# A four-layer kernel's start: the group norm's factors spread by TensorE, eight input buffers, later loads for the second layer, and a first step on VectorE

## The chip, the cores and the metric

One core of a Trainium2 chip runs the whole kernel. The metric is device time in microseconds (us), the median of runs; all values are float32.

## What is computed

The input `x` is 8 images of 16 channels and 128 by 128 points. Four layers follow, each adding its result to what went in, after a group norm (8 groups of two channels). The change concerns the first, an attention layer:

```
x = x + L0(gn(x))                       # then L1, L2, L3 in the same way
# L0, for each point: T = 3 tokens of 48 numbers (the 3x3 patch, wrapped at the edges)
x = fold(in_x); h = ln(x); q, k, v = split(h @ w_attn.T)     # 4 heads of 12
att = softmax(q k / sqrt(12)); x = x + (att v) @ w_proj.T
x = x + gelu(ln(x) @ w_fc.T) @ w_fcp.T
out = conv_w . sum over tokens of ln(x) + conv_b
```

The second layer (16 by 16 products with gates made from means and maxima) needs the weights `w1_0` to `w1_4` and the vectors `b1_0` to `b1_4`.

## The kernel before

**Start.** ScalarE's queue issues one load of constants, then `rep` (L168) and the loop at L219 issue 96 small loads: biases and second-layer weights, each repeated for 8 images. Meanwhile SP's queue loads the input in eight pieces `xj` of 1 MB into two buffers (L236 to L240), and VectorE takes statistics of each (`bn_stats`, L242). `group_stats` (L178) makes from them, per channel and image, the factor `rs` and the shift `d`: aggregate, two small TensorE products (`pm`, `pv`), a square root on ScalarE (L197), and a few VectorE operations. Only then is the table `const0` loaded (L246).

**The factors.** L263 to L275 write `rs` and `d` to DRAM (`aff_d`) and read them back with 24 loads in the layout that the products need, as `aff`. L308 to L324 make `wcen`, the centring weights of four pairs of images, with `aff` in them: four rounds of a POOL memset, two VectorE copies, one TensorE product (`pb`) and one VectorE operation, with two buffers. The layer's own weights (`wqkv`, `wfc`, `wcv`, `wpc`, `wfq`, `wfp`) are loaded on ScalarE's and SP's queues; `centered` (L290) takes the mean off three of them on VectorE.

**The steps.** The layer is worked in 32 steps of four image rows (`Step`, L403). The loop at L656 overlaps them: in turn n, `ahead` (step n + 2) loads its rows into the single buffer `xin` (24 loads, 32 for step 0) and is centred, `then` (n + 1) gets q, k, v, products and scores, `new` (n) attends, projects and starts its hidden layer, `old` (n - 1) ends its hidden layer, `done` (n - 2) is stored (`store`, L584, which loads `xl` first). In the turns n = -2, -1 and 0 only some of these exist, so step 0 has no other step's work beside it.

- `multiply` (L464): q times shifted k, on POOL, eight operations of 3 or 2 x 512 numbers per partition into the five buffers `large`.
- `scores` (L479): TensorE sums them by head into PSUM bank 1, the fifth score into bank 0, which also holds the variances that `Variances.finish` (L392) reads.
- `softmax` (L490), then `attend` (L511), 12 times: three TensorE products spread the weights into banks 1 to 3, VectorE multiplies by v (L518), and POOL adds two of each three results to the first (L527).
- `project` (L529) needs the sums of two k.

[...] `in_turn` (L210) fixes the order of the instructions it is given on each engine as written; the rest is put in place by a scheduler from the program's order. Every load signals one of eight landing semaphores, taken in turn over both queues, and waits until the semaphore's load before it has landed.

Of the kernel before, what the change touches and what calls it, by code (L numbers as in the profile page):

```python
# [9 lines left out]
F32 = mybir.dt.float32  # L10
# [3 lines left out]
PSUM = bass.MemoryType.PSUM  # L14
# [3 lines left out]
BC = B * C  # L18
# [3 lines left out]
NP = B // 2  # L22
# [14 lines left out]
def _constants():  # L37
    g, r = (a.reshape(-1) for a in np.mgrid[0:2, 0:E])
    token = 64 * g + r
    h, c = r // HD, r % C  # L40
    parts = {}
    center = np.zeros((128, 64))
    center[token, r] = 1.0
    center[token, :E] -= 1.0 / E
    parts["center"] = center

    halfvar = np.zeros((128, 62))
    halfvar[token, 30 + g] = -0.5 / E
    parts["halfvar"] = halfvar
    score = np.zeros((128, 56))  # L50
    score[token, 24 + 4 * g + h] = 1.0
    parts["score"] = score
    spread = np.zeros((128, 4, 128))
    bcast = np.zeros((128, 5, 128))
    last = np.zeros((128, 3, 128))
    for t in range(4):
        bcast[32 * t + 16 + g, 4, token] = 1.0
        for n in range(4):
            bcast[32 * t + 4 * (n // 2) + 2 * (n % 2) + g, n, token] = 1.0
            spread[32 * t + 8 * n + 4 * g + h, n, token] = 1.0  # L60
    for k in range(4):
        for u in range(3):
            v = 32 * (2 * (k % 2) + u % 2) + 8 + 4 * (u // 2) + 2 * (k // 2)
            last[v + g, u, 32 * k + 16 * g + c] = 1.0
    parts["spread"] = spread.reshape(128, 512)
    parts["bcast"] = bcast.reshape(128, 640)
    parts["last"] = last.reshape(128, 384)
    p = np.arange(BC)
    parts["pair"] = 0.5 * (p[:, None] // 2 == p[None, :] // 2)


    parts["chan"] = 1.0 * (p[:, None] % 4 == np.arange(4)[None, :])
    gather = np.zeros((128, 2, 2, 32))
    for g in range(2):
        gather[p, 0, g, g * 16 + p % C] = -1.0
        gather[p, 1, g, g * 16 + p % C] = 2.0
    parts["gather"] = gather.reshape(128, 128)
    parts["image"] = 1.0 * (p[:, None] // C == np.arange(B)[None, :])
    parts["basis"] = 3 * (3.5 - (p // C)[:, None])

    copies = np.zeros((128, 2, 128))
    for g in range(2):
        for j in range(8):
            copies[p, g, j * C + p % C] = p // C % 2 == g
    parts["copies"] = copies.reshape(128, 256)
    at, where = 0, {}
    for name, a in parts.items():
        where[name] = (a.shape[0], at, at + a.shape[1])
        at += a.shape[1]
    out = np.zeros((128, at), np.float32)  # L90
    for name, a in parts.items():
        n, lo, hi = where[name]
        out[:n, lo:hi] = a
    return out, where
# [6 lines left out]
def kernel(  # L101
# [63 lines left out]
    eps_t = cpool.tile([128, 1], F32, name="eps")  # L165
    nc.gpsimd.memset(eps_t, EPS)

    def rep(vec, n, name):  # L168

        t = cpool.tile([n * C, 1], F32, name=name)  # L170
        for b in range(n):
            nc.scalar.dma_start(t[b * C : (b + 1) * C], vec.unsqueeze(1))
        return t

    bias0 = rep(b0_conv, B, "bias0")
# [34 lines left out]
    def in_turn(engine, ins):  # L210

        if engine in chain:
            tc.add_manual_dep(ins, chain[engine].name, order, reason="in turn")
        chain[engine] = ins
        return ins
# [3 lines left out]
    for n in range(5):  # L219
        t = cpool.tile([BC, BC], F32, name=f"w1_{n}")  # L220
        nc.gpsimd.memset(t, 0.0)
        for b in range(B):
            r = slice(b * C, (b + 1) * C)
            nc.scalar.dma_start(t[r, r], w1[n].rearrange("i o -> o i") if n < 2 else w1[n])
        w1s.append(t)
        b1s.append(rep(b1[n], B, f"b1_{n}"))

# [5 lines left out]
    x1d = dram.tile([BC, HW], F32, name="x1d")  # L233
    with ExitStack() as l0:
        wp = l0.enter_context(tc.tile_pool(name="w0", bufs=1))
        with tc.tile_pool(name="x0", bufs=2) as xp:  # L236
            bn0 = xp.tile([BC, NCH, 6], F32, name="bn0", bufs=1)
            for j in range(8):
                t = xp.tile([BC, HW // 8], F32, name="xj")
                nc.sync.dma_start(t, xv[:, bass.ts(j, HW // 8)])  # L240
                for i in range(NCH // 8):
                    nc.vector.bn_stats(bn0[:, NCH // 8 * j + i], t[:, bass.ts(i, 512)])  # L242
            mean0, _, rs0, d0 = group_stats(bn0, "0")
        lo, hi = _WHERE["center"][1], _WHERE["last"][2]
        const0 = wp.tile([128, hi - lo], F32, name="const0")
        nc.scalar.dma_start(const0, const_in[:, lo:hi])  # L246

        def k0(name):
            _, a, z = _WHERE[name]
# [7 lines left out]
        def zeros(shape, name):  # L257
            t = wp.tile([128, *shape], F32, name=name)
            nc.gpsimd.memset(t, 0.0)
            return t  # L260


        aff_d = dram.tile([BC, 2], F32, name="aff_d")  # L263
        aff_s = wp.tile([BC, 2], F32, name="aff_s")
        nc.vector.tensor_copy(aff_s[:, 0:1], rs0)
        nc.vector.tensor_copy(aff_s[:, 1:2], d0)
        nc.sync.dma_start(aff_d, aff_s)
        aff = zeros([2, NP], "aff")
        for a in range(2):
            src = aff_d[:, a : a + 1].rearrange("(d p g c) a -> p g c (d a)", p=2, g=2, c=C)  # L270
            for odd in range(2):
                for g in range(2):
                    for i in range(3):
                        r = 64 * (g ^ odd) + 16 * i
                        nc.sync.dma_start(aff[r : r + 16, a, odd::2], src[odd, g])  # L275


        wqkv = zeros([3, 64], "wqkv")
# [2 lines left out]
        for i in range(3):  # L281
            for g in range(2):
                r = slice(64 * g + i * 16, 64 * g + i * 16 + 16)
                nc.scalar.dma_start(
                    wqkv[r, :, :E], w0_qkv[i].rearrange("c (n o) -> c n o", n=3)
                )
                nc.sync.dma_start(wfc[r], w0_fc[i])
                nc.scalar.dma_start(wcv[r, g * 16 : (g + 1) * 16], w0_conv[i])

        def centered(t):  # L290
# [6 lines left out]

        wpc, wfp, wfq = (zeros([64], name) for name in ("wpc", "wfp", "wfq"))
        for g in range(2):
            nc.sync.dma_start(wpc[64 * g : 64 * g + E, :E], w0_proj)  # L300
            nc.scalar.dma_start(wfq[64 * g : 64 * g + 64, :E], w0_fcp[128:192])
        nc.scalar.dma_start(wfp[:, :E], w0_fcp[0:128])
        for t in (wpc, wfp, wfq):
# [19 lines left out]
                    wcen[:, k], center, aff[:, 0, k : k + 1], pb, op0=ALU.mult, op1=ALU.add  # L323
                )  # L324

        xin = wp.tile([128, NP, 512], F32, name="xin")
        nc.gpsimd.memset(xin, 1.0)
        act = l0.enter_context(tc.tile_pool(name="act0", bufs=1))
        tmp = l0.enter_context(tc.tile_pool(name="tmp0", bufs=1))
        ps = l0.enter_context(tc.tile_pool(name="ps0", bufs=1, space=PSUM))  # L330
# [72 lines left out]
        class Step:  # L403
# [57 lines left out]
                    else:  # L461
                        copy(t, p)

            def multiply(self, d):  # L464

                for k in range(2):
                    parts = []
                    for at, n in ((0, 3), (3, 2)):
                        t = large("pd")
                        ins = nc.gpsimd.tensor_mul(  # L470
                            t[:, :n].rearrange("p n (a b) -> p n a b", a=4),
                            rows(self.q[d][:, k]).unsqueeze(1).to_broadcast([128, n, 4, W]),
                            windows(self.k[d][:, 4 * k : 4 * k + 4], at, n),
                        ).ins
                        in_turn("pool", ins)
                        parts += [t[:, i] for i in range(n)]
                    self.pd[2 * d + k] = parts

# [29 lines left out]
                nc.vector.reciprocal(sm, sm)  # L508
                nc.vector.tensor_mul(a, a, sm.unsqueeze(1).to_broadcast([96, 3, 512]))  # L509

            def attend(self, k, j):  # L511

                for u in range(3):
                    r = slice(32 * u, 32 * u + 32)
                    pe(banks[:, 1 + u], spread[r, k], self.att[r, j], start=True, stop=True)
                y = large("y")
                v = self.v[k // 2][:, 4 * (k % 2) : 4 * (k % 2) + 4]
                ins = nc.vector.tensor_mul(  # L518
                    y.rearrange("p n (a b) -> p n a b", a=4),
                    banks[:, 1:4].rearrange("p n (a b) -> p n a b", a=4),  # L520
                    windows(v, j, 3),
                ).ins
                in_turn("dve", ins)
                if j == 0:
                    self.y[k] = y
                else:
                    in_turn("pool", nc.gpsimd.tensor_add(self.y[k], self.y[k], y).ins)  # L527
# [128 lines left out]
        for n in range(-2, NCH + 3):  # L656
# [40 lines left out]
            if ahead:  # L697
                for d in range(2):
                    ahead.load(d)
            ring["from"] = 2 if new else 1  # L700
            for i, fs in enumerate(between):
                if new:
                    new.attend(i // 3, i % 3)
                for f in fs:
                    f()
            ring["from"] = 1
# [2 lines left out]
                    new.project(1, u)  # L709
                new.square(1)  # L710
            if then:
                then.multiply(0)
                then.qkv(1)
                then.multiply(1)
            if ahead:
                ahead.first(var)
            if new:
# [755 lines left out]
```

## Time and profile before

| | us |
|---|---|
| median of 3 runs (11128.83 to 11133.0) | 11128.91 |
| the profiled execution | 11134.61 |
| its span, first to last instruction | 11132.8 |
| busy: PE / VectorE (DVE) / ScalarE (ACT) / POOL | 8824.5 / 9078.7 / 8772.0 / 4922.7 |
| eight POOL products of step 0 (L470) | 103.87 to 126.19 |
| first attend of step 0 | 144.14 |
| first projection of step 0 | 174.15 |

The profile shows one execution. In its rows, times are us from the start of the span unless ns is named. PE is TensorE, PEld its weight load, SP the engine whose queue issues DMAs; "ACTq" and "SPq" are the parts of engines that issue. `out<-in` names the tiles, x4 a count, and square brackets hold the idle time before an instruction and what ended it. A float32 TensorE product stands as two MATMUL pieces. Matmul records can be missing here and there.

### The profile page before, as it was taken

The page shows a single profiled execution, that of the slowest core. Times are in us where ns is not written, and L with a number is a line of the kernel's source. Part 1 is how long each engine was busy: PE and PEld are TensorE (multiplying, and loading weights), DVE is VectorE, ACT ScalarE, POOL GpSimd, SP SyncE. Part 2 cuts the span into 40 slices and gives each one's busy share as a digit, 9 for nine tenths or more (in the row PEclk, how much of TensorE's full clock was granted, in tenths as well). Part 3 has the DMA queues.
Part 4 walks back from the last instruction along what each step waited for, and adds up shares of the span by engine and source line. Part 5 has one row for each costly group of instructions (what it writes and reads, how often), then busy time and mean ns, then how long its engine had stood idle before and what let it go on. Part 6 is the DMA issues. An engine that isn't in the chain of part 4 may idle for free.

```text
span 11132.8 us, 173994 instructions
## 1 busy us (share of the span) xinstructions
PE 8824.5 (79%) x72372; PEld 2092.4 (19%) x72372; DVE 9078.7 (82%) x6829; ACT 8772.0 (79%) x7107; POOL 4922.7 (44%) x2681
## 2 busy tenths in 40 slices
PE   5999999999997677777777777777777777777799
PEld 1222222222222111111111111111111111111122
DVE  3555555555555699999999999999999999999977
ACT  2555555555545699999999999999999999999988
POOL 3555555555553734433343343344344333443421
PEclk8999999999998799999999999999999999999999
DMA  1000000000002300000000000000000000000022
GB/s 48 13 15 13 14 13 15 14 13 13 15 6 79 129 15 7 7 13 7 7 10 10 7 7 13 7 7 13 7 7 7 13 7 7 13 7 7 2 61 62
DMA packets 189390, 203.91 MB, mean 18 GB/s; under 512 B 46776, under 2 KB 155448, under 8 KB 186552
## 3 DMA queue, kind: packets, MB, share of 16 engines
q1 hardware_dynamic: 179944, 190.68, 6.2%
q8 instruction: 569, 9.32, 0.3%
q10 hardware_dynamic: 8656, 2.11, 0.1%
q14 instruction: 221, 1.81, 0.1%
HBM read 107.15 MB, written 60.04 MB: 15 GB/s over the span
## 4 chain that ended last, share of the span: by engine, by line
DVE 45%; PE 31%; ACT 14%; issue 5%; POOL 2%; DMA 1%; SPq 1%; DVEq 0%; ACTq 0%; POOLq 0%
DVE t L1003 22%; PE banks L360 18%; DVE u L1009 14%; PE pn L971 10%; ACT t L992 9%; DVE y L518 2%; PE acc L1322 1%; POOL y L527 1%; DVE x L538 1%; PE pd L971 1%; ACT hid L152 1%; ACT u L152 1%; DMA yd<-y 1%; DVE x L630 1%; DVE p L1162 1%
## 5 line engine op out<-in xcount | busy, mean ns | idle before, releaser
L971 PE MATMUL pn<-f,wa 32*64 32x512 f32 x18432 | 3419.6, 625 | 1711.3 <-DVE u L1009 1668.7
L1024 POOL TENSOR_TENSOR v<-t,u 128x1024 f32<-128x1024 f32 x1152 | 2738.1, 2377 | 4020.4 <-DVE t L1003 3860.0
L1009 DVE TENSOR_TENSOR u<-pn,u 128x1024 f32<-128x1024 f32 x2304 | 2715.5, 1220 | 117.7
L971 PE MATMUL pd<-f,wb 32*64 32x512 f32 x18432 | 2600.7, 626 | 157.0 <-ACT t L992 91.7
L1003 DVE SCALAR_TENSOR_TENSOR t<-t,u 128x2048 f32<-128x2048 f32 x1152 | 2631.3, 2284 | 34.2 <-ACT u L152 34.0
L992 ACT ACTIVATE t<-pd 128x1024 f32<-128x1024 f32 x2304 | 2338.2, 1015 | 313.8 <-PE pn L971 307.1
L152 ACT ACTIVATE u<-t 128x2048 f32<-128x2048 f32 x1152 | 2202.9, 1912 | 53.0 <-PE acc L1055 17.4
L152 ACT ACTIVATE u<-u 128x2048 f32<-128x2048 f32 x1152 | 2190.8, 1902 | 0.0
L971 PEld LDWEIGHTS pn<-f,wa 32*64 32x64 f32 x18432 | 751.0, 131 | 3774.7 <-DVE u L1009 3246.5
L1016 DVE SCALAR_TENSOR_TENSOR u<-t,u 128x1024 f32<-128x1024 f32 x1152 | 1420.1, 1233 | 37.6
L152 ACT ACTIVATE hid<-banks 128x1024 f32<-128x1024 f32 x576 | 571.8, 1023 | 1049.9 <-PE banks L360 1048.1
L527 POOL TENSOR_TENSOR y<-y 128x1536 f32<-128x1536 f32 x256 | 894.6, 3494 | 834.4 <-DVE y L518 834.4
L1055 PE MATMUL acc<-u,const 128*32 128x512 f32 x9216 | 1257.4, 618 | 1.9 <-DVE u L1016 1.9
L518 DVE TENSOR_TENSOR y<-banks,vp 128x1536 f32<-128x1536 f32 x384 | 673.2, 1753 | 274.7 <-PE banks L360 271.6
L544 ACT ACTIVATE sq<-x 128x1024 f32<-128x1024 f32 x384 | 398.0, 1054 | 412.4 <-DVE x L538 289.8
L470 POOL TENSOR_TENSOR pd<-q,kp 128x1536 f32<-128x1536 f32 (+1 forms) x256 | 693.4, 2731 | 8.0 <-PE banks L360 6.3
L971 PEld LDWEIGHTS pd<-f,wb 32*64 32x64 f32 x18432 | 514.6, 132 | 753.5 <-ACT t L992 691.9
L360 PE MATMUL banks<-att,const 32*128 32x512 f32 x2304 | 498.8, 668 | 173.7 <-DVE att L509 95.9
L360 PE MATMUL banks<-h,wfc 64*128 64x512 f32 (+1 forms) x3072 | 620.8, 633 | 14.5 <-DVE h L606 14.5
L1055 PE MATMUL acc<-v,const 128*32 128x512 f32 x4608 | 616.5, 606 | 0.2 <-POOL v L1024 0.2
L606 DVE TENSOR_TENSOR h<-banks,x 128x1024 f32<-128x1024 f32 x192 | 232.5, 1211 | 438.0 <-ACT hid L152 227.6
L360 PE MATMUL banks<-rstd,const 32*128 32x512 f32 (+1 forms) x1216 | 411.5, 641 | 19.4 <-DVE rstd L400 15.1
(181 smaller groups left out, 7337.0 us busy)
## 6 DMA issues: line engine op xcount, KB each, us to landing
f<-yd SPq DMA_DIRECT2D x512, 101.6 KB
yd<-y SPq DMA_DIRECT2D x320, 130.0 KB
xin<-in_x SPq DMA_DIRECT2D x752, 32.0 KB
four<-sil SPq DMA_DIRECT2D x256, 65.0 KB
xj<-in_x SPq DMA_DIRECT2D x8, 1024.0 KB
xl<-in_x SPq DMA_DIRECT2D x32, 256.0 KB
x1d<-xl SPq DMA_DIRECT2D x32, 256.0 KB
x<-x1d SPq DMA_DIRECT2D x8, 1024.0 KB
```

The lines of the kernel that those rows point to most:

```text
L152: ins = nc.scalar.activation(out_, in_, func, **kw).ins
L360: in_turn("pe", mm(*args, skip_group_check=True, **kw).ins)
L470: ins = nc.gpsimd.tensor_mul(t[:, :n].rearrange("p n (a b) -> p n a b", a=4), rows(self.q[d][:, k]).unsqueeze(1).to_broadcast([128, n, 4, W]),
L518: ins = nc.vector.tensor_mul(y.rearrange("p n (a b) -> p n a b", a=4), banks[:, 1:4].rearrange("p n (a b) -> p n a b", a=4), windows(v, j, 3),
L527: in_turn("pool", nc.gpsimd.tensor_add(self.y[k], self.y[k], y).ins)
L971: yield mm(p[64 * (u % 2) : 64 * (u % 2) + 64, u // 2], w[lo : lo + 32, q % 2, n].rearrange("p c f -> p (c f)"), fs[g * NP + q][lo : lo + ...
L992: in_turn("act", nc.scalar.activation(self.t[:, ab], self.pd.pop(ab), AF.Abs).ins)
L1003: ins = nc.vector.scalar_tensor_tensor(self.t, self.t, 1.0, self.u, op0=ALU.add, op1=ALU.mult).ins
L1009: ins = nc.vector.tensor_mul(self.u[:, ab], self.pn.pop(ab), self.u[:, ab]).ins
L1016: ins = nc.vector.scalar_tensor_tensor(r, self.t[:, :, 0], 2.0, r, op0=ALU.subtract, op1=ALU.mult).ins
L1024: ins = nc.gpsimd.tensor_mul(self.v, self.t[:, :, 1], self.u[:, :, 1]).ins
L1055: ins = mm(accs[k][32 * q : 32 * q + 32], gather[:, int(part == 1), g], (c.u[:, ab, 0], c.u[:, ab, 1], c.v[:, ab])[part], start=first, sto ...
```

## The change

- **Factors.** A selection matrix `pick` and a mask `pairs` are added to the constants. VectorE multiplies `pairs` by `rs` and by `d` into `both`; two TensorE products with `pick` put the factors where `aff` wants them, and one VectorE copy takes them out of PSUM. The trip through DRAM goes.
- **Input.** The `x0` pool has eight buffers instead of two. `const0` (now 1978 columns, 1718 before) is loaded ahead of the pieces, on ScalarE's queue; the memset of `xin` is moved ahead too.
- **Loads.** The 96 small loads are gathered in a list and issued on SP's queue in turn n = 0, behind the row loads of step 2. `wfc` and `wpc` go from SP's to ScalarE's queue.
- **First step.** `multiply` runs on VectorE when there is no `new` (step 0 alone). `attend` uses banks 4 to 6 instead of 1 to 3 for every second of the first seven attends when there is no `old` (step 0 alone).

```diff
+    pick = np.zeros((128, 2, 128))
+    for odd in range(2):
+        for i in range(3):
+            pick[p, odd, 64 * (p // C % 2 ^ odd) + 16 * i + p % C] = 1.0
+    parts["pick"] = pick.reshape(128, 256)
+    parts["pairs"] = 1.0 * (p[:, None] // 32 == np.array([0, 2, 1, 3])[None, :])
...
+    loads = []
...
-            nc.scalar.dma_start(t[b * C : (b + 1) * C], vec.unsqueeze(1))
+            loads.append((t[b * C : (b + 1) * C], vec.unsqueeze(1)))
...
-            nc.scalar.dma_start(t[r, r], w1[n].rearrange("i o -> o i") if n < 2 else w1[n])
+            loads.append((t[r, r], w1[n].rearrange("i o -> o i") if n < 2 else w1[n]))
...
-        with tc.tile_pool(name="x0", bufs=2) as xp:
+        lo, hi = _WHERE["center"][1], _WHERE["last"][2]
+        const0 = wp.tile([128, hi - lo], F32, name="const0")
+        nc.scalar.dma_start(const0, const_in[:, lo:hi])
+        xin = wp.tile([128, NP, 512], F32, name="xin")
+        nc.gpsimd.memset(xin, 1.0)
+        with tc.tile_pool(name="x0", bufs=8) as xp:
...
-        nc.sync.dma_start(aff_d, aff_s)
-        aff = zeros([2, NP], "aff")
...
-                        nc.sync.dma_start(aff[r : r + 16, a, odd::2], src[odd, g])
+        nc.vector.tensor_scalar_mul(both[:, 0], k0("pairs"), rs0)
+        nc.vector.tensor_scalar_mul(both[:, 1], k0("pairs"), d0)
+        with tc.tile_pool(name="ps_aff", bufs=1, space=PSUM) as pp:
+            pa = pp.tile([128, 2, 2, NP // 2], F32, name="pa")
+            pick = k0("pick").rearrange("p (o m) -> p o m", o=2)
             for odd in range(2):
+                src = both[:, :, 2 * odd : 2 * odd + 2]
+                mm(pa[:, odd], pick[:, odd], src, start=True, stop=True)
+            nc.vector.tensor_copy(
+                aff.rearrange("p a (d o) -> p a d o", o=2), pa.rearrange("p o a d -> p a d o")
+            )
...
-                nc.sync.dma_start(wfc[r], w0_fc[i])
+                nc.scalar.dma_start(wfc[r], w0_fc[i])
...
-            nc.sync.dma_start(wpc[64 * g : 64 * g + E, :E], w0_proj)
+            nc.scalar.dma_start(wpc[64 * g : 64 * g + E, :E], w0_proj)
...
-                        ins = nc.gpsimd.tensor_mul(
+                        ins = (nc.vector if engine == "dve" else nc.gpsimd).tensor_mul(
...
-                    pe(banks[:, 1 + u], spread[r, k], self.att[r, j], start=True, stop=True)
+                    pe(banks[:, at + u], spread[r, k], self.att[r, j], start=True, stop=True)
...
+            if n == 0:
+                for dst, src in loads:
+                    nc.sync.dma_start(dst, src)
...
-                    new.attend(i // 3, i % 3)
+                    new.attend(i // 3, i % 3, 4 if not old and i < 7 and i % 2 else 1)
...
-                then.multiply(0)
+                then.multiply(0, "pool" if new else "dve")
                 then.qkv(1)
-                then.multiply(1)
+                then.multiply(1, "pool" if new else "dve")
```

More of the change, by code (lines that the diff above doesn't have):

```diff
@@ L64, in _constants @@
             last[v + g, u, 32 * k + 16 * g + c] = 1.0
+    p = np.arange(BC)
+    pick = np.zeros((128, 2, 128))
[4 more added lines that the diff above has]
+    parts["pairs"] = 1.0 * (p[:, None] // 32 == np.array([0, 2, 1, 3])[None, :])
     parts["spread"] = spread.reshape(128, 512)
@@ L67, in _constants @@
     parts["last"] = last.reshape(128, 384)
-    p = np.arange(BC)
     parts["pair"] = 0.5 * (p[:, None] // 2 == p[None, :] // 2)
@@ L243 @@
             mean0, _, rs0, d0 = group_stats(bn0, "0")
-        lo, hi = _WHERE["center"][1], _WHERE["last"][2]
-        const0 = wp.tile([128, hi - lo], F32, name="const0")
-        nc.scalar.dma_start(const0, const_in[:, lo:hi])
         def k0(name):
@@ L260, in zeros @@
             return t
[L263 to L266, printed above, removed]
-        nc.sync.dma_start(aff_d, aff_s)
-        aff = zeros([2, NP], "aff")
-        for a in range(2):
-            src = aff_d[:, a : a + 1].rearrange("(d p g c) a -> p g c (d a)", p=2, g=2, c=C)
-            for odd in range(2):
[L272 to L275, printed above, removed]
+        aff = wp.tile([128, 2, NP], F32, name="aff")
+        both = wp.tile([128, 2, NP], F32, name="both")
+        nc.vector.tensor_scalar_mul(both[:, 0], k0("pairs"), rs0)
[3 more added lines that the diff above has]
+            pick = k0("pick").rearrange("p (o m) -> p o m", o=2)
+            for odd in range(2):
+                src = both[:, :, 2 * odd : 2 * odd + 2]
[3 more added lines that the diff above has]
+            )
         wqkv = zeros([3, 64], "wqkv")
@@ L324 @@
                 )
-        xin = wp.tile([128, NP, 512], F32, name="xin")
-        nc.gpsimd.memset(xin, 1.0)
         act = l0.enter_context(tc.tile_pool(name="act0", bufs=1))
@@ L462, in qkv, with multiply @@
                         copy(t, p)
-            def multiply(self, d):
+            def multiply(self, d, engine):
                 for k in range(2):
@@ L474, in multiply @@
                         ).ins
-                        in_turn("pool", ins)
+                        in_turn(engine, ins)
                         parts += [t[:, i] for i in range(n)]
@@ L509, in softmax, with attend @@
                 nc.vector.tensor_mul(a, a, sm.unsqueeze(1).to_broadcast([96, 3, 512]))
-            def attend(self, k, j):
+            def attend(self, k, j, at):
                 for u in range(3):
                     r = slice(32 * u, 32 * u + 32)
-                    pe(banks[:, 1 + u], spread[r, k], self.att[r, j], start=True, stop=True)
+                    pe(banks[:, at + u], spread[r, k], self.att[r, j], start=True, stop=True)
                 y = large("y")
@@ L519, in attend @@
                     y.rearrange("p n (a b) -> p n a b", a=4),
-                    banks[:, 1:4].rearrange("p n (a b) -> p n a b", a=4),
+                    banks[:, at : at + 3].rearrange("p n (a b) -> p n a b", a=4),
                     windows(v, j, 3),
```

## The prediction

> **What bounds the kernel now.** I read the page first. Its chain of work (part 4) runs through every layer, and the diff touches only what comes before the loop over steps and, inside it, branches that are true for the first step alone (`n == 0`, `not old`, `new` is None). The changed program's instruction order agrees: from the second step on, TensorE, VectorE and ScalarE have the rows of before. So the question is what the first 208 us of 11132.8 are worth, and I read the waits from 0 to 100 us:
>
> ```profile
> ACT L152 <- DMA b<-in_b: 60.2, 1, 60.2
> DVE s L199 <- ACT s L152: 13.5, 1, 13.5
> DVE bn L242 <- DMA xj<-in_x: 24.6, 8, 6.2
> ```
>
> ScalarE's square root (its variance is ready at 48.25) waits until 61.49, because 97 loads, 80 of them for the second layer, stand in front of it on ScalarE's own queue. VectorE waits 24.6 us for the eight input pieces. The timeline of that stretch gives the milestones:
>
> ```profile
> 42.60 2.47 DVE L242 BATCH_NORM_STATS2 bn<-xj 128x6 f32<-128x512 f32 x4 [1.56 <-DMA xj<-in_x]
> ...
> 60.19 1.28 ACT L152 ACT_TABLE_LOAD   x1 [60.19 <-DMA b<-in_b]
> ...
> 67.49 13.01 SPq L275 DMA_DIRECT2D aff<-aff_d  x24
> ...
> 82.25 0.14 DVE L317 COPY shift<-aff 64x1 f32<-64x1 f32 x1 [1.40 <-DMA aff<-aff_d]
> ...
> 85.35 3.75 PE L360 MATMUL banks<-xin,wcen 64*64 64x512 f32 x16 [0.38 <-DVE wcen L322]
> ```
>
> Statistics end at 45.07, the factors travel through DRAM from 62.94 to 82.25, and the first centring product runs at 85.35. From there the timelines of PE, DVE and POOL show step 0:
>
> ```profile
> 115.44 10.75 POOL L470 TENSOR_TENSOR pd<-q,kp 128x1536 f32<-128x1536 f32 x4
> ...
> 126.24 1.92 PE L360 MATMUL banks<-pd,const 128*32 128x512 f32 x4 [0.38 <-POOL pd L470]
> ...
> 142.33 1.75 DVE L509 TENSOR_TENSOR att<-att,mx 96x1536 f32<-96x1536 f32 x1
> ...
> 144.14 2.08 PE L360 MATMUL banks<-att,const 32*128 32x512 f32 x6 [15.98 <-DVE att L509]
> 148.18 2.08 PE L360 MATMUL banks<-att,const 32*128 32x512 f32 x6 [1.96 <-DVE y L518]
> ```
>
> POOL's products end the wait before the softmax (126.19, last score 128.16). Then each attend waits for VectorE to empty the banks of the one before: a period of 4.0 us, eight times. The table by stretch adds TensorE's clock (columns: window, length, then busy time of PE, PEld, DVE, ACT, POOL with counts, granted clock, DMA share, GB/s):
>
> ```profile
> 144.00:174.00 30.00, 16.45 (x48) 4.13 (x48) 12.39 (x8) 0.00 (x0) 13.69 (x4) 0.50 0.00 1
> ```
>
> All times below are of this execution (11132.8 span, 11134.6 in all, 1.8 outside the span). The median of the runs is 11128.9, 5.7 lower; I subtract the same gain from it.
>
> **Input and statistics.** "Eight at once" is only partly so. A landing semaphore is taken in turn from eight, over both queues, and a load waits for its semaphore's previous load. In the changed order piece 3 waits for piece 1, piece 4 for piece 3, piece 8 for piece 5, and pieces 5 to 7 for small loads on ScalarE's queue, which themselves wait for pieces 1 to 3. One piece alone took about 4.7 us (issued 10.51, its statistics at 15.27). The first two and the first constant, 2.37 MB, had landed by 9.05; with 1.01 MB more of constants now beside them, at some 0.4 MB/us (the DMA rows of 0 to 12 us), pieces 1 and 2 land at 6.3 and 11.4, 3 and 4 at 14 and 18.7, and from 18 us four overlap: piece 8 lands at about 31.2, against 42.6.
>
> VectorE does not follow at once: its order puts the centring of `wfp` and `wfq` in front of piece 5's statistics, and `wfp` is ScalarE's 25th load, issued near 21.1. Alone it took 2.04 us (74.34 to 76.38), which gives 23.2; under the pieces a small load took 4.18 to 6.11 us in the chain of the first 62 us, and five weight loads are queued in a row, so at the latest it lands with the last piece, 31.5. [...] The 4.2 to 6.1 us row is nearer and gives 29.5, which I take. Then four pieces at 2.47 and 0.5 of centring: statistics end at 39.9 (33.7 by the early end, 41.9 by the rule).
>
> **Factors.** Aggregate to variance is 3.14 as before (45.11 to 48.25). The square root no longer queues: its 25 loads are issued by 22 and the table load has no wait, so 0.05 instead of 13.2. Root to `d` 1.23 as before: 44.4. Added: two small VectorE scalings (0.4 with their turn-round), two matmuls of the kind of `pm` (0.58 each, 1.1), one copy (0.16): 46.1. The trip through DRAM, 62.94 to 82.25, is gone. The four `wcen` rounds stay, 3.3 (the last two took 3.0): 49.4. What is late next is `xin`: its 8th load waits for piece 8 (31.2), 24 more at 0.57 (32 took 18 us) and 2.04 to land make 46.9 for the second half; no wait, but one of about 1.3 us if statistics end early. First product: 85.35 to 49.4, gain **36** (34 to 41).
>
> **Products on VectorE.** Eight POOL products end at 126.19. VectorE's price is L509's, both inputs in SBUF: 1.75 for 1536, so 1.2 for 1024. On the clock of before: two products from 103.9 to 106.9, then `hn` (1.23), held back from 104.41 to 106.9. That is the added wait: `hn` queues behind two products, and TensorE's q, k, v of the second half queue behind it, 2.5 late; `kp` is then wrapped at 111.9. Two more products fit before that, two follow to 114.9, a third to 116.6, then the `rstd` pair to 118.1. TensorE's fifth score shares `rstd`'s bank, so it and ten more wait for 118.1, and the last product needs its buffer. Twelve matmuls at 0.35 (the score row at 112.67: 1.06 for three) or at 0.64 (the row at 126.24: 1.92 for the last ones, at half the clock) end at 122.3 to 125.8. TensorE has idled 4 us by then, so I take five at half the clock and seven at the full one: 124.0 against 128.16. Gain **4** (2.4 to 5.9), though VectorE itself is 10 us quicker than POOL. POOL's `vp` wraps may be held one product, 1.75; they aren't needed until the attends.
>
> **Attends in two sets of banks.** Period of before 2.08 + 1.77 + turn-round. With alternating banks, attends 0 to 6 run back to back and the 8th starts at 16.5 instead of 28.0 after the first. But POOL's additions take 3.46 each, need one and the same accumulator in turn, and four of them precede the projection: second y at 6.0, then 9.5, 13.0, 16.5, 20.0. The projection started at 30.0 (174.15), so the gain is **10**, POOL ends the wait and not TensorE. [...] Since POOL holds TensorE idle before the projection, I keep 10.
>
> **Loads moved to SP.** 96 loads at 0.47 (56.43: eight in 3.73) are 45 us of SP's queue, behind step 2's `xin` (issued by 83) and ahead of step 0's `xl` and step 3's `xin`: done near 128. Step 3's centring stood at 286.17, now 236. Cover 236 - 128 - 9.3 = 98 us: cost 0. The eight weight loads moved from SP to ScalarE are in the 25 above. Larger constants (1978 columns for 1718) are in the 1.01 MB; the `xin` memset (1.80) delays ScalarE's third load to 3.6, behind constants still flowing.
>
> **Sum:** 36 + 4 + 10 = 50. Profiled 11134.6 becomes 11084.6; the median 11128.9 becomes 11079. Nothing later has a fixed time, so the lead should last to the end.
>
> **Rivals.** *Weights in time* (15%): `wfp` lands near 23; gain 41 + 4 + 10, 11074. Against it: the slow small loads. *No overlap of pieces* (12%): semaphores keep pieces in single file and statistics still end at 45; the root's 13.2 and the DRAM trip go all the same (40.3 becomes 9.5), gain 30.8 + 14, 11084. *The lead is lost later* (5%): an engine that was waiting for something else than step 0 in steps 1 and 2; nothing in the waits speaks for it; with half lost 11104. *SP's queue becomes the bound* (3%), the slower side: from 1.5 us per moved load step 3's input is late, from 2.0 the whole gain is gone; at 2.3, with 4-byte rows and each load waiting on a landing, 83 + 221 + 9.3 is 77 us past 236, so 27 more than before: 11156. Against it: the same loads took 0.62 each among the pieces. The sum as worked out: 65%.
>
> **Numbers.** Predicted 11079; range 11065 to 11092, from the high ends (41 + 5.9 + 12, and a few us by a higher TensorE clock) to the low ends (30.8 + 2.4 + 9.9, less noise), leaving out the two rare cases and a little of each side. About 0.2%, 22 us, is what a measurement can tell. Faster 0.93, same 0.04, slower 0.03.
>
> **What would show it.** First centring product at 44 to 52; no `aff_d`; the square root right after the variance; fifth piece's statistics starting after `wfp`; first attend 16.0 after the last score as now, step 0's attends 2.1 apart, POOL additions back to back, projection about 20 after the first attend; SP's moved loads done before 150. Wrong if the time from the first product of step 3 to the end changes by more than a few us, or if statistics end past 45.

## The result, and the profile after

The changed kernel takes 11093.76 us (median of 7 runs, 11090.65 to 11094.79) where before takes 11128.83 beside it (median of 7): a ratio of 0.9968, 95% interval 0.9957 to 0.998. That is 35 us less, where 50 were predicted, and 1.8 above the predicted range. The profiled execution took 11093.76 with a span of 11091.7; against the span of 11132.8 in the profile of before that is 41.1 less.

The waits of after from 0 to 100 us (engine, line and what it waited for; us in total, times, longest):

```profile
ACT s L159 <- DVE var L204: 20.7, 1, 20.7
...
DVE bn L257 <- DMA xj<-in_x: 12.3, 4, 6.7
...
DVE csum L305 <- DMA wpc<-in_w_proj: 6.3, 1, 6.3
...
DVE csum L305 <- DMA wfp<-in_w_fcp: 3.0, 1, 3.0
```

The square root now waits for its variance and no longer for a queue; VectorE waits for four pieces, and then for two weights. The timeline of VectorE shows where these weights stand:

```profile
19.72 2.47 DVE L257 BATCH_NORM_STATS2 bn<-xj 128x6 f32<-128x512 f32 x4 [2.54 <-DMA xj<-in_x]
28.48 0.20 DVE L305 TENSOR_REDUCE csum<-wpc 128x1 f32<-128x48 f32 x1 [6.29 <-DMA wpc<-in_w_proj]
...
31.89 0.20 DVE L305 TENSOR_REDUCE csum<-wfp 128x1 f32<-128x48 f32 x1 [3.02 <-DMA wfp<-in_w_fcp]
...
32.51 2.46 DVE L257 BATCH_NORM_STATS2 bn<-xj 128x6 f32<-128x512 f32 x4
...
35.22 7.21 DVE L257 BATCH_NORM_STATS2 bn<-xj 128x6 f32<-128x512 f32 x12
...
46.73 0.16 DVE L215 SCALAR_TENSOR_TENSOR d<-mean,rs 128x1 f32<-128x1 f32 x1
```

Four pieces are worked as they land. Then nothing happens from 22.2 to 28.5, and the last four pieces run without a wait, so they had landed by the time VectorE came to them. Statistics end at 42.43 (45.07 in before), `d` stands at 46.89 (62.72). TensorE's timeline carries on:

```profile
52.31 4.22 PE L370 MATMUL banks<-xin,wcen 64*64 64x512 f32 x16 [0.38 <-DVE wcen L334]
...
84.01 6.80 PE L370 MATMUL banks<-pd,const 128*32 128x512 f32 x24 [3.82 <-DVE rstd L410]
105.98 3.79 PE L370 MATMUL banks<-att,const 32*128 32x512 f32 x12 [15.17 <-DVE att L519]
110.03 3.79 PE L370 MATMUL banks<-att,const 32*128 32x512 f32 x12 [0.26 <-DVE y L528]
...
123.98 4.68 PE L370 MATMUL banks<-y,wpc 64*64 64x512 f32 x16
128.59 1.13 PE L370 MATMUL banks<-att,const 32*128 32x512 f32 x6
```

The attends come in pairs (x12 where before had x6 and 1.96 us of idle time each), and the attend after the projection starts at 128.59, where before had it at 177.59. So step 0's end is **49.0** us earlier, 1 less than the sum. The lead is lost later. To see where, I cut every trace at the same VectorE instructions, counted back from the end, and took the lengths between them, with the time in which TensorE's granted clock was 0.50 behind the slash ("layer 3" is 4050 to 10520 on before's clock):

| us / of it at clock 0.50 | to 300 | to 1000 | to 1900 | to 3300 | layer 3 | span |
|---|---|---|---|---|---|---|
| before | 299.1 / 82 | 701.3 / 38 | 899.6 / 31 | 1399.6 / 48 | 6470.6 / 113 | 11132.8 |
| after | 249.8 / 65 | 701.1 / 38 | 899.0 / 27 | 1403.6 / 58 | 6476.5 / 133 | 11091.7 |
| lead won | 49.3 | 0.2 | 0.6 | -4.0 | -5.9 | 41.1 |

(The parts left out, 3300 to 4050 and the last 612 us, add 0.9.) For 1600 us behind the changed front the lead stands within 0.8; then 4.0 goes in one place, and 5.9 in a layer that the diff does not touch.

### The profile page after: what moved, and what is told of

Same layout as the page of the kernel before. It is cut to its first block, busy times and chain, and to the rows that moved or that the text cites. A ratio compares the mean times of both kernels' runs of the same rounds, so it can differ in the third digit from the quotient of the medians.

```text
span 11091.7 us, 173967 instructions
## 1 busy us (share of the span) xinstructions
PE 8838.5 (80%) x72376; PEld 2098.5 (19%) x72376; DVE 9089.0 (82%) x6838; ACT 8770.5 (79%) x7107; POOL 4906.6 (44%) x2672
## 4 chain that ended last, share of the span: by engine, by line
DVE 45%; PE 30%; ACT 14%; issue 5%; POOL 2%; SPq 1%; DMA 1%; DVEq 0%; ACTq 0%; POOLq 0%
DVE t L1017 22%; PE banks L370 18%; DVE u L1023 14%; PE pn L985 10%; ACT t L1006 9%; DVE y L528 2%; POOL y L537 1%; DVE x L548 1%; ACT u L159 1%; PE pd L985 1%; PE acc L1336 1%; ACT hid L159 1%; DMA yd<-y 1%; DVE p L1176 1%; DVE x L640 1%
## 5 line engine op out<-in xcount | busy, mean ns | idle before, releaser
L480 POOL TENSOR_TENSOR pd<-q,kp 128x1536 f32<-128x1536 f32 x248 | 672.0, 2735 | 8.4 <-PE banks L370 7.5
```

The costliest lines, as they stand in the source:

```text
L480: ins = (nc.vector if engine == "dve" else nc.gpsimd).tensor_mul(t[:, :n].rearrange("p n (a b) -> p n a b", a=4), rows(self.q[d][:, k]).un ...
```

## The experiments

Theories: **A**, the stretches in which TensorE's granted clock is 0.50 (3.41 or 6.83 us each; from 1000 to 3000 us 14 in before, 15 in after) fall elsewhere against the work after a head start, so that it is not carried one for one. **B**, the profiled execution of before was a long one. **C**, the change moved the layers' tiles in memory. **D** was formed after the first four kernels: the length of VectorE's program ahead of a loop decides which of its instructions start late. That these stand where blocks of the program end, as the expectations put it, was a guess.

**Before, again** (no edit).

> The kernel before, unchanged, for a second profile. Theory A (a head start is not carried one for one, because the stretches in which TensorE's granted clock is 0.50 fall differently behind it): the first attend starts within 1 us of 144.14, the steps up to 1800 us lie within 1 us of the first profile's, and the end scatters by several us with the total of half-clock time. Theory B (the profiled execution of before was itself a long one, and the typical one is nearer 11124): the profiled execution lies 4 us or more below 11134.6, and the difference shows at one place. Theory C (placement in memory by the change slows the later layers): this kernel tells nothing on it, and repeats 11132.8 us of span within 1 us. Time against before: 0 within 4 us.

Measured: 11133.8 (median of 11; before beside it 11131.9), span 11133.0. Front 296.9 where it was 299.1, layer 3 6471.9. The end did not follow the front's 2.2 us; no other stretch scatters by more. B fails: the second profile is as long as the first.

**First-only**: products on VectorE and two sets of banks, put into before.

```diff
-                        ins = nc.gpsimd.tensor_mul(
+                        ins = (nc.vector if engine == "dve" else nc.gpsimd).tensor_mul(
...
-                    new.attend(i // 3, i % 3)
+                    new.attend(i // 3, i % 3, 4 if not old and i < 7 and i % 2 else 1)
```

> Before with two parts of the change alone: step 0's products on VectorE and two sets of banks for step 0's attends. By the trace of after the first attend starts 5.1 us earlier than in before and attend 8 a further 10.8 us earlier, so the front's lead is about 16. Theory A: the end gains 16 less or more by up to some 6 us, the loss falling in places where the half-clock stretches differ. Theory C (placement): the end gains the whole 16 within 1 us, as no tile of the later layers moves. One for one: 11113 where before is 11129.

Measured: 11115.1 against 11131.9 (ratio 0.9986, 0.9977 to 0.9995): 16.8. Front 282.1, that is 17.0 under the first before and 14.8 under its repeat. These two parts bring what their rows said, and carry it to the end.

**Loads-only**: the 96 loads moved, in before.

```diff
+            if n == 0:
+                for dst, src in loads:
+                    nc.sync.dma_start(dst, src)
```

> Before with one part of the change alone: the 96 loads of the second layer's weights go from ScalarE's queue to SyncE's in step 0. In before sqrt ends at 61.49 behind variance at 48.25, in after 0.03 behind it; so the first centring product should come 13 us earlier (72 in place of 85.35), and the factors still cost what they cost in before. Front's lead 13. One for one the time is 11116 where before is 11129; Theory A allows 6 us to either side; if the loads on SyncE's queue held up step 1's input, the lead at step 1's products would be below 10.

```profile
42.75 0.16 DVE L207 SCALAR_TENSOR_TENSOR d<-mean,rs 128x1 f32<-128x1 f32 x1
```

```profile
62.14 3.57 PE L362 MATMUL banks<-xin,wcen 64*64 64x512 f32 x12 [0.38 <-DVE wcen L324]
```

The first fence is VectorE's timeline, the second TensorE's. Measured: the first centring product at 62.14, 23.2 earlier and not 13, since the weights and the pieces land sooner too; with two buffers `d` stands earlier (42.75) than in after. The median, 11119.8, is only 12.1 below before's. The profiled execution was the fastest of 11 (11104.5), so its trace does not stand for the median, which is 15.3 longer; where the other executions spend that, no trace shows. In the profiled one the stretch to 1000 took 696.3 with 27 us at 0.50, 5.0 less than every other kernel's. That is Theory A, in the kernel's favour. But its layer 3 took 6477.9, as in after, and no tile had moved: C cannot be the cause there.

**Centring-late**: in after, the centring of `wpc`, `wfp` and `wfq` tied behind the statistics.

```diff
+            held = nc.vector.tensor_copy(stat.tile([BC, 1], F32, name="held"), d0).ins
...
-            nc.vector.tensor_reduce(s, t[:, :E], AX.X, ALU.add)
+            ins = nc.vector.tensor_reduce(s, t[:, :E], AX.X, ALU.add).ins
+            tc.add_manual_dep(ins, held.name, order, reason="later")
```

> After, with the centring of the three small weight matrices tied behind the statistics of all eight pieces on VectorE, so that no wait for a weight's landing stands between two pieces' statistics. In after VectorE waited 6.29 us to 28.48 for one of the weights and 3.02 to 31.89 for the next, while five or more pieces had landed by then. Statistics end at 33 to 36 in place of 42.43, the first centring product at 45 to 48 in place of 52.31 (the weights' centring, some 3 us, may then stand in the path for part of it). Front's lead over after: 5 to 8. One for one the time is 6 us below after's; Theory A lets the end differ from that by up to 6 us.

Measured: 11088.2 (median of 5), 5.6 below after's first median; the first centring product at 46.44, 5.9 earlier. VectorE's timeline:

```profile
28.23 5.03 DVE L257 BATCH_NORM_STATS2 bn<-xj 128x6 f32<-128x512 f32 x8 [1.69 <-DMA xj<-in_x]
33.73 2.47 DVE L257 BATCH_NORM_STATS2 bn<-xj 128x6 f32<-128x512 f32 x4 [0.47 <-DMA xj<-in_x]
```

Statistics end at 36.2 with no weight between pieces. The wait for `wpc` and `wfp` cost after 6 us.

These four traces gave the clue. In layer 3 of after VectorE's product `u` from `pn` sometimes starts late; this is its timeline there:

```profile
7740.18 2.36 DVE L1023 TENSOR_TENSOR u<-pn,u 128x1024 f32<-128x1024 f32 x2
7742.57 1.23 DVE L1030 SCALAR_TENSOR_TENSOR u<-t,u 128x1024 f32<-128x1024 f32 x1
7743.71 2.28 DVE L1017 SCALAR_TENSOR_TENSOR t<-t,u 128x2048 f32<-128x2048 f32 x1
7746.45 2.35 DVE L1023 TENSOR_TENSOR u<-pn,u 128x1024 f32<-128x1024 f32 x2 [0.46 <-DVE t L1017]
```

In layer 3 of after the first `u` starts 0.10 after `t` ends in 1070 of 1087 rounds. In the other 17, as here, it takes 0.46 or 0.47, though it waits for nothing but VectorE's own `t`. There are 16 such gaps in loads-only, 17 in centring-late (at the same instructions as in after), and none in before, its repeat and first-only. In loads-only, whose program is six entries shorter, each stands one round later. 17 times 0.36 is 6.1 us: the layer's 5.9. In the built program, counting VectorE's entries from 0, with the waits that stand as instructions of their own (its separate waits), every one of these instructions stands at an entry that leaves 64 when divided by 128. All 17 of after stand there, and none of the other 1070 does. The page's part 3 has this line:

```profile
q14 instruction: 219, 1.79, 0.1%
```

That is 219 packets of 8.2 KB; the trace holds 28250 records of all engines but TensorE, 129 for each packet. That the packets carry the programs of these engines, in blocks of 128 entries, is an estimate from this count alone. VectorE's program has 10145 entries in before, 10153 in first-only, 10148 in loads-only, 10154 in after and in centring-late (each trace holds two records fewer). A round of layer 3 has six entries, so steps of 128 fall on every second place of it: with the odd lengths these are the separate waits ahead of `t` and of `u`, and the second `u`; with the even ones the first `u` itself, right behind its wait, then `u` from `t`, and `t`. If Theory D is right, one more instruction takes the gaps away or brings them.

**After, one more; before, one more; centring-late, one more; after, again.** The edit of the first three:

```diff
+                if j == 0:
+                    nc.vector.bn_stats(bn0[:, 0], t[:, bass.ts(0, 512)])
```

> After, with one more instruction on VectorE: the statistics of the first piece's first 512 columns twice, in the wait for the second piece. What it tests: in the third layer VectorE's product u from pn starts 0.46 us after t in place of 0.10, without a wait on another engine, 17 times in after, in the centring-late kernel and 16 times in loads-only, and never in before, its repeat and first-only; the places are the same instructions in each run and stand 86, 172 or 600 of VectorE's instructions apart. Theory D (where the blocks of VectorE's program end, which shifts by one instruction, makes this gap; the even or odd length of what comes before decides): no such gap is left, the third layer (4050 to 10520) takes 6470 to 6473 us in place of 6476.5, and the time is 6 us below after's, about 11088. Theory A (clock stretches only): the gaps stay, and the time is after's within 3 us.

> Before, with the same one more instruction on VectorE in the wait for the second piece. Theory D: 16 or 17 gaps of 0.46 us appear in the third layer, which takes 6476 to 6479 us in place of 6470.6, and the time is 6 us above before's. Theory A: no such gap, and before's time within 4 us.

> The centring-late kernel (11088.2) with the same one more instruction on VectorE. Theory D: no gap of 0.46 us in the third layer, and 6 us less: about 11082, the lowest of all kernels here. Theory A: 11088 within 3 us.

> After unchanged, for a second profile and for its time beside the others. Theory D: the same 17 gaps at the same instructions. Theory A for the stretch from 1900 to 3300 us, where the profile of after has 58.0 us at a clock of 0.50 and takes 1403.6 us, and before has 47.8 and takes 1399.6: if the pattern comes from where after's steps begin, it repeats within 1 us; if it is a matter of the single execution, the stretch may as well take 1396 to 1400. Time 11092 within 3.

| | program entries | to 3300, from 1900 | layer 3 | gaps | median |
|---|---|---|---|---|---|
| before beside them | 10145 | 1399.6 | 6470.6 | 0 | 11125.4 |
| before, one more | 10146 | 1396.2 | 6476.3 | 18 | 11134.9 |
| after, again | 10154 | 1403.6 | 6474.8 | 17 | 11094.2 |
| after, one more | 10155 | 1400.2 | 6470.1 | 0 | 11082.9 |
| centring-late | 10154 | 1403.6 | 6478.7 | 17 | 11088.2 |
| centring-late, one more | 10155 | 1400.2 | 6470.2 | 0 | 11077.6 |

(Before's stretches are those of its first profile; centring-late's median was taken with the first four kernels, where before's was 11131.9.) One more VectorE instruction, 0.68 us long and hidden under a load, takes the gaps from after and 11.3 us with them (the slowest run with it is faster than the fastest without), and gives before 18 gaps. Before's 9.5 us are less sure: its ratio's interval, 0.9998 to 1.0016, does not exclude that nothing changed. Centring-late with one more is the fastest kernel here (ratio to before 0.9957, 0.9944 to 0.9971). The same place in "after, one more":

```profile
7728.94 2.36 DVE L1025 TENSOR_TENSOR u<-pn,u 128x1024 f32<-128x1024 f32 x2
7731.33 1.22 DVE L1032 SCALAR_TENSOR_TENSOR u<-t,u 128x1024 f32<-128x1024 f32 x1
7732.47 2.28 DVE L1019 SCALAR_TENSOR_TENSOR t<-t,u 128x2048 f32<-128x2048 f32 x1
7734.86 2.35 DVE L1025 TENSOR_TENSOR u<-pn,u 128x1024 f32<-128x1024 f32 x2
```

No idle time stands before the last line. The gain was larger than the 6 expected, and a part of it stands in the table: in both pairs made from after the stretch to 3300 gets 3.4 us shorter too. The rest of the 11.3 is not located; between single traces the spans differ by 7.4 (after's first profile) and 2.3 (its second, the fastest of its 6 runs). In the pair from before the stretch to 3300 got shorter as well, by 3.4, against the sign: of its 9.5 the traces show 5.7 in layer 3. The traces of "after, again" and "after, one more" keep a distance of 2.96 us from 1000 on. It becomes 2.81 at 2491.89, where `x` stands at entry 1600 right behind a separate wait, and stays at 2.81 to 2.83 until the following instruction, here in "after, again":

```profile
2686.57 1.22 DVE L454 TENSOR_TENSOR hn<-banks,xc 128x1024 f32<-128x1024 f32 x1
2691.85 2.35 DVE L548 TENSOR_TENSOR x<-banks,xc 128x1024 f32<-128x1024 f32 x2 [4.07 <-PE banks L370]
```

and here in "after, one more":

```profile
2689.39 1.21 DVE L456 TENSOR_TENSOR hn<-banks,xc 128x1024 f32<-128x1024 f32 x1
2694.32 2.35 DVE L550 TENSOR_TENSOR x<-banks,xc 128x1024 f32<-128x1024 f32 x2 [3.71 <-PE banks L372]
```

TensorE's products for it start at 2690.30 and 2693.12, 2.82 apart like what stands just before; but `x` starts 0.36 later in the first. It is entry 1728 of the program, again 64 above a multiple of 128 and again right behind a separate wait. From there the half-clock stretches differ: 3.4 at 2744.2, 6.8 at 2843.2 and 6.8 at 2945.6 in the first, 6.8 at 2743.7 and 3.4 at 2948.5 in the second, 6.8 us more in the first, whose steps fall behind by 3.1 more up to 2953. So these late starts come just before the pattern of A tips, which speaks for them as its cause. A is right in this: the pattern repeats in after's second profile (1403.6, 58.0), as it said for a pattern set by where the steps begin.

**Loads-back, two buffers, a control with two more, and before a third time.** Loads-back is after with the 96 loads on ScalarE's queue at the start again; the next two edits are

```diff
-        with tc.tile_pool(name="x0", bufs=8) as xp:
+        with tc.tile_pool(name="x0", bufs=2) as xp:
```

and the one more instruction above, twice.

> After, with the 96 loads of the second layer's weights back on ScalarE's queue at the start. Queue: sqrt waits again until about 61 (61.49 in before, 45.65 in after), the first centring product comes at about 68 in place of 52.3, the front loses 16, and the time is about 11109. Theory D: VectorE's program is 10150 entries long here, waits counted, and the entry 64 of a block of 128 falls on the first product u from pn 17 times, so the gaps of 0.46 us stay although the loads are back where they were in before: it is the length of what comes before, and not the queue of the loads. If the gaps vanish, Theory D is wrong and the move itself makes them.

> After, with two buffers for the input's pieces in place of eight (VectorE's program keeps its 10154 entries, so the gaps of 0.46 us stay). If sending all pieces at once brought a part of the gain, statistics end some 3 us later than in after and after's repeat (42.4 and 39.4): about 44, and the time is 3 us more. If it brought nothing, as loads-only (two buffers, statistics ending at 38.5) suggests, statistics end at 38 to 42 and the time is after's within 3 us.

> Control for the one more instruction: after with the statistics of the first piece's first 512 columns three times, two instructions more (10156 entries). Theory D: two more leave the waits and the work on the same side of the blocks' ends, the gaps of 0.46 us stay at 17 or so, and the time is after's within 3 us (11092 to 11094), 11 us above that with one more. If any added instruction there brought the gain of the one more (11082.9), the time is about 11083.

> Before unchanged, a third profile: its two profiled executions took 11134.6 and 11134.7, and the medians of its runs lay at 11128.8, 11131.9 and 11125.4. If the profiled execution is one of the shorter ones, the table by stretches shows where the shorter runs save: the first 300 us (299.1 and 296.9 so far), a step pattern with fewer stretches at a clock of 0.50 (as loads-only had in its first 1000 us), or the third layer. No gap of 0.46 us in the third layer. Time 11129 within 4.

Loads-back: 11116.9 (before beside it 11129.8), worse than the 11109 expected. ScalarE's timeline:

```profile
61.38 1.28 ACT L159 ACT_TABLE_LOAD   x1 [61.38 <-DMA b<-in_b]
...
77.89 1.02 ACT L367 ACTIVATE xc<-banks 128x1024 f32<-128x1024 f32 x1 [15.02 <-DMA xin<-in_x]
```

The square root waits to 62.67, the first centring product comes at 71.17 and not at 68: `const0` stands behind the 96 loads, and so do the weight loads, the last of them issued at 77.17, and ScalarE's own `xc` comes after them in its order, whatever releaser its row names. The front is 24.6 longer than in after. There are 17 gaps again, at other rounds, as the program is four entries shorter than after's, and layer 3 takes 6479.9. The loads are where before has them: the move as such does not make the gaps. The stretch to 3300 takes only 1400.3 here, and 1399.6 in loads-only, though both lengths are even: that part of the loss does not follow odd or even alone.

Two buffers: 11093.1, statistics ending at 41.4. Eight pieces at once brought nothing that shows. Two more (10156 entries): 11094.6, 17 gaps, at entries 64 above multiples of 128, and 1403.6 for the stretch to 3300. So an added instruction alone does not help; one helps and two do not. In this kernel `x` stands right behind a separate wait at entries 1216 and 1344, and starts late there (1881.73 and 2085.66). It is 1.40 us ahead of "after, one more" behind the first and 1.94 behind it at 2347: the loss of 3.3 moved with the entries, 600 us earlier than in after. Before, third: 11132.3, no gap, layer 3 6470.3, front 298.0.

## Why the prediction was wrong

**Start, 36.** It brought 33.0 (85.35 to 52.31), just under its low end. `wfp` landed at 31.9, where the estimate for the latest, a landing with the last piece, was 31.5 and the row I chose gave 29.5. I also had `wfp` as the first weight in VectorE's way; `wpc` was, at 28.48. Statistics ended at 42.43 for 39.9. But one trace does not decide between the two ends for `wfp`, for in after's second profile it was there by 28.81:

```profile
28.50 0.20 DVE L305 TENSOR_REDUCE csum<-wpc 128x1 f32<-128x48 f32 x1 [7.20 <-DMA wpc<-in_w_proj]
...
28.81 0.20 DVE L305 TENSOR_REDUCE csum<-wfp 128x1 f32<-128x48 f32 x1
```

Statistics ended at 39.35 there and the first centring product came at 49.22, 36.1 earlier than in before. So this term was off only by what it scatters from execution to execution. The sum's "41.9 by the rule" is the latest end, 31.5, carried on; no run shows a rule that holds a small load back behind a whole piece, and the two profiles of after have 42.43 and 39.35 in its place. The factors held: 0.03 to the square root for 0.05, 5.42 from `d` to the product for 5.0. The eight buffers carried none of it that shows (two buffers cost nothing); the queue that the 96 loads had filled carried most (the first centring product 23.2 earlier in loads-only, and 18.9 later than after's in loads-back).

**Products, 4.** 5.1: the last of TensorE's scores ended 37.4 and the first attend began 38.16 us earlier. The sum's term is the first of these, 4.3; the other 0.8 lies between the last score and the first attend, which the prediction had as unchanged (15.17 of idle time, 15.98 in before). VectorE's eight products, with `hn` and `rstd` between, were done at 87.2, 34.9 behind the centring product; the order was as predicted. The split of the last twelve scores into five at half the clock and seven at the full one was an estimate; in after they ran from 84.01 to 90.81, at a mean granted clock of 0.56 up to 87.4 and at 1.00 behind it.

**Attends, 10.** 10.8 up to the attend behind the projection, with TensorE at 0.50 up to 127.95; the row of before has 0.50 too. The table by stretch for this place in after (columns: window, length, busy time of PE, PEld, DVE, ACT, POOL with counts, granted clock, DMA share, GB/s):

```profile
106.00:124.00 18.00, 15.47 (x50) 4.42 (x50) 12.18 (x7) 0.00 (x0) 12.18 (x4) 0.50 0.04 2
```

TensorE is now busy for 15.47 of 18 us and still at 0.50. The range's high end has 12 for the attends, and a few us by a higher TensorE clock; no run shows these terms. In after the granted clock stayed at 0.50 until 127.95, 22 us after the first attend began. The projection started 18.0 after the first attend, not 20: its first products follow the eighth attend without a wait, and only its second half waits for POOL, whose fourth addition ends at 125.51. So the gain of 12.0 at its start shrinks to 10.8, as it takes 4.68 for before's 3.51.

**"Loads moved to SP", 0.** The queue was right: issued from 79.04 to 124.9, nobody waits. What was missed is what the move and the rest do to a program's length, a thing that the prediction had no term for.

**"Nothing later has a fixed time, so the lead should last to the end"** is the step that failed. The lead was 49.0 after step 0, against 50. Then, in the first pair of traces, 4.0 went in the steps near 2700 to 3000 and 5.9 in layer 3. The prediction's own sign of being wrong, a time behind step 3's first product that changes by more than a few us, came true.

The part in layer 3, about 6, is shown: 17 late starts, since VectorE's program became 9 entries longer, an odd number. They go with one more instruction, are there with two more, and come to before with one. The part in the steps, 3.4 to 4.0, is shown for the kernels made from after: it goes with one more and is there with two more, at other steps. Before with one more, loads-only and loads-back have even lengths and no such loss, so what it hangs on is the place of the late starts in the steps, as far as is known. With one more, the lead by traces is 48.5 (11132.8 to 11084.3) and by medians 42.6 (11125.4 to 11082.9).

The rival "the lead is lost later" had 5% and a wrong place for it: the steps 1 and 2, where nothing was lost.

**Left open.** All 93 runs of before together have a median of 11130.2, all 13 of after 11093.8: 36.4. Step 0 leads by 49 and the program's length takes about 10, which the first pair of traces adds up to its 41.1; of the medians some 3 us are not located. The medians of before moved from 11125.4 to 11131.9 between the groups of runs, so this may be no more than their spread. Why only an entry right behind a separate wait shows the delay was not tried. For `t` the trace of after suggests a reason: its separate wait is over 0.04 us after the `u` before it has started, more than 1 us before `t` itself can start, so a delay of 0.36 would be hidden, while the wait ahead of the first `u` ends only when `t` does. For `u` from `t`, which has no separate wait, it stays open. That the place 64 above a multiple of 128 is where a block of the program ends is a guess from the packet count and the spacing; no run shows it.

## What to carry to other kernels

Before counting on a gain at the front to last to the end, look for an engine without slack in a long unrolled loop. A change in the number of instructions ahead of it cost 0.36 us here at 17 of the 51 steps of 128 entries in layer 3. One idle instruction more, with two more as the control, shows whether that is so. Compare two traces stretch by stretch between the same instructions, not only their ends: a loss in code that was not edited shows at once. A load moved off a queue is judged by all that stood behind it (24.6 us of the front in loads-back), and a buffer count only where a piece waits for a buffer (two took 11093.1 where eight took 11093.8).

## What the hardware showed that was not expected

- **One entry in 128.** An instruction of VectorE that stands 64 above a multiple of 128 entries and right behind a separate wait started 0.36 us late, 17 times in layer 3 of after. One VectorE instruction more moved layer 3 by 5.7 us in before and by 4.7 to 6.4 in after.
- **Half-clock stretches lock to the steps.** In before and after they are 3.41 or 6.83 us long from 1000 to 3000 us, some 99 to 205 us apart, and the 11 from 300 to 1800 us of before come 49.4 us earlier in after, each with its length; in "first-only" and before the stretches from 300 to 1900 are the same ones 17 us apart. In after, a shift of 0.36 us (0.5 with the one at entry 1600) was followed by another pattern for some 210 us.
- **POOL beside VectorE's products.** POOL's small wraps of `vp`, 0.20 us each for `kp`, took up to 1.19 us while VectorE multiplied two tiles from SBUF (`pd`, from 70.50 on):

```profile
70.40 0.20 POOL L470 COPY kp<-kp 128x16 f32<-128x16 f32 x1
71.60 0.72 POOL L469 COPY vp<-vp 128x16 f32<-128x16 f32 x1 [1.00 <-ACT vp L367]
72.26 1.19 POOL L470 COPY vp<-vp 128x16 f32<-128x16 f32 x1
```

With POOL doing its own products in before, each of these wraps of `vp` took 0.20. They were not on the path here.
